# Packed bf16 down weights by converting DMAs, three down products per group moved forward, the verdict counted in two parts and the last output cut in the middle, in a state-space and fp8 FFN kernel

## Chip, cores and metric

The kernel runs on one core of a Trainium2 chip. The metric is the device time of one execution in microseconds (us). A core has five engines with instruction streams of their own: TensorE (matmuls; PE in the profile, its weight loads PEld), VectorE (DVE), ScalarE (ACT), GpSimd (POOL) and SyncE (SP). They run side by side and wait for each other through semaphores. DMAs are issued by SP (its queue is q1 in the profile) and by POOL (q0), and 16 DMA engines serve both queues.

## The reference

x has the shape (B, H, L) = (128, 32, 512) in f32. The reference computes

```
K    = state-space kernel, (H, L), from log_dt, C, log_A_real, A_imag   # 64 complex modes
y    = causal convolution of x[:, h, :] with K[h] + x * D, masked to length[b]
g, u = fp8(y) @ gate_w.T * s_g,  fp8(y) @ up_w.T * s_u        # 512 -> 1376, fp8(): clip to +-448, round to e4m3
hid  = silu(g) * u
out  = x + fp8(hid) @ down_w.T * s_d                          # 1376 -> 512
```

The three weights hold fp8 values, stored as f32 with one scale each.

## The kernel before, in words

The 32 heads are worked in G = 8 groups of HG = 4 heads, 512 (head, row) columns per group. I = 1376 is padded to IC = 11 chunks of 128. The program first makes the convolution kernels K in three batches of heads (class `Powers`), writes them to DRAM (`kpad`) and reads them back, per head, as Toeplitz tiles `st` (`toeplitz`, L475 and L476).

One group goes through these stages:

- `conv` (L572): for each head 6 f32 matmuls with `st` (L490 to L499), then VectorE writes the masked fp8 tile `q` (L576, L586). `sort` (L589) permutes the rows by length on TensorE, and ScalarE copies the result to `qs` (L601).
- `gate_up` (L630): for each of the 11 chunks 4 gate and 4 up matmuls (L646), ScalarE's silu (L654), VectorE's product `v` (L656). Chunks are quantised in batches of one or two (`quantise`, L615): ScalarE's magnitude `m` (L621), then three VectorE steps (L622, L623, L624) that write the bf16 tile `hq`. There are seven such jobs. Three are done inside `gate_up`, the other four are put between the convolutions of the next group, and the last two of these cover chunks 9 and 10.
- `Down` (L672): for each head 11 matmuls `dp` (L689), one per chunk, with a [128, 128] piece of `hq` as weights and 512 columns of `dm` as moving data; `put_out` (L698) adds the scaled result to `xn` on VectorE (L702) and sends rows to `out` with an indirect DMA on POOL's queue (L707).

The order is written out by hand: `with after(x)` puts what follows behind `x` on its engine. In group g's loop body (from L765), after `gate_up` of group g, TensorE gets: two convolutions of group g+1; chunks 0 to 4 (EARLY = 5) of heads 0 and 1; the other two convolutions and sorts; chunks 5 to 8 (LATE = 9) of heads 0 and 1; two sorts; chunks 0 to 8 of head 2 (L818); and then, at L819 to L825, chunks 9 and 10 of heads 0, 1 and 2 and all 11 of head 3. Chunk 10 waits for the last quantisation job. In group G-2 = 6 head 3 is left for the next group's time (L831). The last group's head 3 is worked in two halves of 256 columns (`halves`, L764), its products come batch by batch (L840 to L850), and `verdict` is put behind the third head's.

The PSUM tiles have tags with two banks each: `gp`, `up`, `cp`, `dp`. In `Down` heads 0 and 1 use `dp`, heads 2 and 3 use `cp` (as the convolutions do).

Weights: gate, up and down are loaded as f32 with SP's DMAs and stay in SBUF (`gw`, `uw`, `dw`). As all values fit in bf16, matmuls read the upper halves with a step of two bf16 (L570). down is loaded behind x of group 1 in two parts (L740, L741). The assumption is checked: `low_halves` (L535) lets ScalarE sum the lower halves of each chunk (4 + 4 + 11 sums, four per group from group 0 on, L805), and `verdict` (L548) collects these sums and checks of overflow, equal scales and row counts in the tile `ok`; a matmul with `ones` (L561) adds up over partitions, and `any_bad` (L562) is loaded by all engines (L923). If it is set, the slow path `wide` runs, else all engines branch past it (L924) to the end of the program (L970).

Besides, POOL issues the loads of `xs` (L111, and L112, which accumulates), the gathers of `xn` (L464), and in group 0 the write of `kpad` for batch 1 (L334) and the `st` loads of group 1.

## Time and profile before

| | us |
|---|---|
| median of 3 runs | 305.42 (304.99 to 305.79) |
| profiled execution | 304.11 |
| its span, from the first to the last instruction | 302.3 |
| DVE busy | 264.3 (87% of the span) |
| PE busy | 282.8 (94%) |
| ACT busy | 180.9 (60%) |
| POOL busy | 51.1 (17%) |
| granted TensorE clock, mean | 0.989 |

The profile is of one execution. Its page gives the busy time of each engine, the chain of work that ended last, the costliest groups of instructions and the DMAs. The trace behind it answers finer questions: the chain in order of time, timelines of one engine in a window (start, us, what, count, idle time before and who ended it), waits, and the instructions of one line or tile. A busy PE isn't PE at its peak: matmuls are pipelined, so the record of one is longer than its distance to the next. Instructions of the sequencers (waits, branches, register loads; SPq, PEldq) are not counted as busy.

### The profile page before, as it was taken

The numbers are of one execution on the slowest core, as the hardware profiler recorded it, in microseconds if no ns is written. First come the engines' busy times: TensorE is split into PE (matmuls) and PEld (weight loads), VectorE is DVE, ScalarE is ACT, GpSimd is POOL, SyncE is SP. The second block draws the span as 40 slices with busy tenths as digits, with TensorE's granted clock in tenths as the row PEclk, the third lists the DMA queues.
The fourth block names the chain that finished last, engine by engine and source line by source line (L and its number), as shares of the span: only waits on it lengthen the run. The fifth ranks groups of instructions, "written<-read, shape, count | busy, mean of one in ns | idle before, by whom it ended". The sixth has DMA issues, their size and how long they took to land.

```text
span 302.3 us, 4827 instructions
## 1 busy us (share of the span) xinstructions
PE 282.8 (94%) x1691; PEld 171.6 (57%) x1708; DVE 264.3 (87%) x466; ACT 180.9 (60%) x385; POOL 51.1 (17%) x105
## 2 busy tenths in 40 slices
PE   8999999997999999999999999999999999999940
PEld 3477567454774557645774567555774567455420
DVE  5875999989999999969997899969996999899970
ACT  5964882977739783657736782738523891579200
POOL 5771440210002100030002100310003100010030
PEclk9999999999999999999999999999999999999995
DMA  2599999970159603793149503890259530020031
GB/s 82 200 264 382 380 360 348 269 280 18 28 133 252 252 1 58 183 304 127 29 133 265 239 1 89 236 327 12 57 133 300 184 129 0 0 105 3 0 128 55
DMA packets 26119, 47.95 MB, mean 159 GB/s; under 512 B 2864, under 2 KB 15420, under 8 KB 24296
## 3 DMA queue, kind: packets, MB, share of 16 engines
q1 hardware_dynamic: 21784, 26.28, 29.4%
q0 software_dynamic: 4304, 21.29, 20.2%
q8 instruction: 15, 0.25, 0.3%
q14 instruction: 16, 0.13, 0.1%
HBM read 39.03 MB, written 8.54 MB: 157 GB/s over the span
## 4 chain that ended last, share of the span: by engine, by line
DVE 45%; PE 28%; issue 12%; ACT 8%; DMA 3%; SPq 1%; POOL 1%; ACTq 0%; POOLq 0%
DVE v L656 11%; DVE v L622 11%; PE dp L689 10%; DVE hq L623 10%; PE gp L646 5%; DVE q L576 5%; ACT s L654 5%; PE up L646 4%; DVE hq L624 4%; ACT m L621 2%; DVE xn L702 2%; DMA st<-kpad 2%; PE cp L497 1%; PE cp L495 1%; PE cp L496 1%
## 5 line engine op out<-in xcount | busy, mean ns | idle before, releaser
L689 PE MATMUL dp<-dw,hq 128*128 128x512 bf16 (+1 forms) x347 | 81.1, 380 | 2.5 <-DVE hq L624 0.8
L654 ACT ACTIVATE s<-gp,psc 128x512 f32<-128x512 f32 x88 | 58.4, 679 | 30.7 <-PE gp L646 30.4
L646 PE MATMUL up<-qs,uw 128*128 128x512 fp8e4 (+1 forms) x352 | 70.3, 322 | 2.3 <-DVE v L656 1.8
L656 DVE SCALAR_TENSOR_TENSOR v<-up,psc,s 128x512 f32<-128x512 f32 x88 | 64.5, 747 | 7.7 <-ACT s L654 7.7
L646 PE MATMUL gp<-qs,gw 128*128 128x512 fp8e4 (+1 forms) x352 | 70.5, 322 | 0.6 <-ACT qs L601 0.6
L689 PEld LDWEIGHTS <-hq 128*128 128x128 bf16 x363 | 33.3, 96 | 42.5 <-DVE hq L624 5.2
L623 DVE SCALAR_TENSOR_TENSOR hq<-m,v 128x1024 bf16<-128x1024 bf16 (+1 forms) x56 | 55.6, 993 | 1.1
L622 DVE SCALAR_TENSOR_TENSOR v<-m,v 128x1024 f32<-128x1024 bf16 (+1 forms) x56 | 55.4, 990 | 1.2 <-ACT m L621 1.2
L621 ACT ACTIVATE m<-v 128x1024 bf16<-128x1024 f32 (+1 forms) x56 | 48.7, 870 | 8.9 <-DVE v L656 8.9
L646 PEld LDWEIGHTS <-uw 128*128 128x128 bf16 x352 | 32.1, 97 | 28.9 <-issue 3.8
L646 PEld LDWEIGHTS <-gw 128*128 128x128 bf16 x352 | 31.9, 97 | 26.4 <-issue 0.7
L601 ACT ACTIVATE qs<-pq 128x376 fp8e4<-128x376 f32 x32 | 14.6, 479 | 29.7 <-PE pq L593 29.7
L702 DVE SCALAR_TENSOR_TENSOR xn<-dp,nsc,xn 128x512 f32<-128x512 f32 (+1 forms) x33 | 23.0, 730 | 8.8 <-PE dp L689 8.8
L493 ACT ACTIVATE shared<-sp,inv 128x128 f32<-128x128 f32 x32 | 11.3, 360 | 27.6 <-PE sp L490 27.6
L576 DVE SCALAR_TENSOR_TENSOR q<-cp,inv,shared 128x512 fp8e4<-128x512 f32 x32 | 23.8, 744 | 1.5 <-PE cp L499 1.0
L707 POOL DMA_INDIRECT out<-xn,index x10 | 10.5, 1051 | 75.4 <-DVE xn L702 71.9
L111 POOL DMA_DIRECT2D xs<-xT x6 | 3.5, 586 | 116.4 <-PE sp L490 116.4
L624 DVE TENSOR_SCALAR hq<-hq 128x1024 bf16<-128x1024 bf16 (+1 forms) x56 | 20.9, 373 | 1.4
L495 PE MATMUL cp<-st,xg 128*128 128x256 f32 x64 | 19.2, 381 | 0.0
L497 PE MATMUL cp<-st,xg 128*128 128x256 f32 x64 | 19.1, 381 | 0.0
L496 PE MATMUL cp<-st,xg 128*128 128x256 f32 x64 | 19.0, 380 | 0.0
L607 ACT ACTIVATE s<-q 128x1024 bf16<-128x1024 fp8e4 x16 | 16.7, 1054 | 0.0
(159 smaller groups left out, 283.6 us busy)
## 6 DMA issues: line engine op xcount, KB each, us to landing
xg<-xT SPq DMA_DIRECT2D x8, 1024.0 KB, 7.4
st<-kpad SPq DMA_DIRECT2D x28, 192.0 KB, 3.8
st<-kpad SPq DMA_DIRECT2D x28, 128.0 KB, 4.0
xs<-xT POOLq DMA_DIRECT2D x12, 256.0 KB, 5.3
dw<-downT SPq DMA_DIRECT2D x2, 1280.0 KB, 19.8
gw<-gateT SPq DMA_DIRECT2D x2, 768.0 KB, 8.2
gw<-gateT SPq DMA_DIRECT2D x1, 1216.0 KB
uw<-upT SPq DMA_DIRECT2D x1, 1216.0 KB, 15.2
```

Of the source, the lines that this page charges most:

```text
L495: nc.tensor.matmul(cp[:, 1:4:2, :], xg[:, 0, b], st[:, 2:4, :], start=True, stop=False)
L497: nc.tensor.matmul(cp[:, 1:3, :], xg[:, 1, b], st[:, 3:5, :], start=False, stop=False)
L576: nc.vector.scalar_tensor_tensor(q[:, j, :].rearrange("p (k c l) -> p k c l", k=2, c=2), cp.rearrange("p (k c) l -> p k c l", k=2), inv[:, ...
L621: nc.scalar.activation(m, v, AF.Abs, scale=2.0**20 * (1.0 + 2.0**-6), accum_out=acc)
L622: yield nc.vector.scalar_tensor_tensor(v, m, 1.5 * 2.0**14, v, ALU.max, ALU.add)
L623: yield nc.vector.scalar_tensor_tensor(out, m, 1.5 * 2.0**14, v, ALU.max, ALU.subtract)
L624: yield nc.vector.tensor_scalar(out, out, FP8_MAX, -FP8_MAX, ALU.min, ALU.max)
L646: multiplied = nc.tensor.matmul(o[:, :, 0 : CAPS[c]], w[:, c, i * P : (i + 1) * P], qs[:, :, OFF[c] : OFF[c] + CAPS[c]], start=(c == 0), s ...
L654: gated = nc.scalar.activation(s, gp, AF.Silu, scale=pgate)
L656: done = nc.vector.scalar_tensor_tensor(v[:, (i - i0) * T : (i - i0 + 1) * T], up, pup, s, ALU.mult, ALU.mult)
L689: done = nc.tensor.matmul(self.dps[n], self.hq[:, i, j * B : (j + 1) * B], dm[:, i, l0:l1], start=(i == 0), stop=(i == IC - 1),)
L702: added = nc.vector.scalar_tensor_tensor(o, self.dps[n], ndown, o, ALU.mult, ALU.add)
```

## The change

- `dw` (f32) becomes `dm` (bf16, packed). POOL loads it with DMAs that convert f32 to bf16: chunks 0 to 4 behind the write of `kpad` of batch 1, then the `st` loads of the four heads of group 1, then chunks 5 to 10. SP no longer loads down there.
- For the check of the lower halves, f32 chunks of down are loaded once more into a staging tile of four buffers (`stage_down`), on SP's queue behind x of group g+2 in groups 1, 2 and 3. ScalarE sums them there, as many sums as before.
- In groups 0 to 5, chunks 0 to 2 of head 3 are multiplied right behind head 2's chunks 0 to 8 (`ahead`), and are left out of head 3's later run.
- `verdict` is divided: `hold_others` counts all checks but `big` behind the first of the last group's remaining jobs, where group 6's last output is put too; `hold_big` counts `big` behind the last job; the matmul over partitions comes behind the first head's products, and `all_hold` compares behind the second head's output.
- The last group's output is sent as heads 0 and 1 and heads 2 and 3, where it was heads 0 to 2 and head 3.

The diff, without the slow path `wide`, which now loads down itself:

```diff
@@ -128,20 +128,22 @@
     x0 = load_x(0)
     gw = const.tile([P, LC, IP], F32, name="gw")
     uw = const.tile([P, LC, IP], F32, name="uw")
-    dw = const.tile([P, IC, L], F32, name="dw")
+
+    dm = const.tile([P, IC, L], BF16, name="dw")
     FI = I // P
 
     def load_gate_up(w, src, i0, i1, queue=nc.sync):
         return queue.dma_start(w[:, :, i0:i1], src[:, i0:i1].rearrange("(c p) i -> p c i", p=P))
 
-    def load_down(i0, i1, queue=nc.sync):
+    def load_down(w, i0, i1, queue):
         if i0 < FI:
-            queue.dma_start(
-                dw[:, i0 : min(i1, FI), :],
+            done = queue.dma_start(
+                w[:, 0 : min(i1, FI) - i0, :],
                 downT[i0 * P : min(i1, FI) * P, :].rearrange("(c p) l -> p c l", p=P),
             )
         if i1 > FI:
-            queue.dma_start(dw[0 : I - FI * P, FI, :], downT[FI * P :, :])
+            done = queue.dma_start(w[0 : I - FI * P, FI - i0, :], downT[FI * P :, :])
+        return done
 
 
     I1, I2, IH = 2 * P, 3 * P, 6 * P
@@ -434,7 +436,7 @@
         if IP > I:
             nc.gpsimd.memset(gw[:, :, I:], 0.0)
             nc.gpsimd.memset(uw[:, :, I:], 0.0)
-            nc.gpsimd.memset(dw[I - FI * P :, FI, :], 0.0)
+            nc.gpsimd.memset(dm[I - FI * P :, FI, :], 0.0)
         for kt in kts[1:]:
             nc.gpsimd.memset(kt, 0.0)
         nc.gpsimd.tensor_scalar(number, col_f[:, B:], -1.0, B - 1.0, ALU.mult, ALU.add)
@@ -535,31 +537,67 @@
     def low_halves(pool):
 
         n = 0
-        for w in (gw, uw, dw):
-            F = w.shape[2]
-            for c in range(w.shape[1]):
-                junk = pool.tile([P, T], F32, name="s")
-                nc.scalar.activation(
-                    junk.bitcast(U8)[:, 0:F], w.bitcast(U16)[:, c, 0 : 2 * F : 2], AF.Copy, accum_out=low[:, n : n + 1]
-                )
+
+        def summed(w, F, rows=P):
+            junk = pool.tile([P, T], F32, name="s")
+            return nc.scalar.activation(
+                junk.bitcast(U8)[0:rows, 0:F],
+                w.bitcast(U16)[0:rows, 0 : 2 * F : 2],
+                AF.Copy,
+                accum_out=low[0:rows, n : n + 1],
+            )
+
+        for w in (gw, uw):
+            for c in range(LC):
+                yield summed(w[:, c, :], IP)
                 n += 1
-                yield
-
-    def verdict(behind):
-        nf, nb, nl = fin.shape[1], big.shape[1], low.shape[1]
-        ok = chk.tile([P, nf + nb + nl + LC], F32, name="ok")
-        nc.vector.tensor_scalar(ok[:, 0:nf], fin, 3.0e38, None, ALU.is_lt)
-        nc.vector.tensor_scalar(ok[:, nf : nf + nb], big, 3.0e38, None, ALU.is_lt)
-        nc.vector.tensor_scalar(ok[:, nf + nb : nf + nb + nl], low, 0.0, None, ALU.is_equal)
-        nc.vector.tensor_copy(ok[:, nf + nb + nl : nf + nb + nl + 1], same)
-        nc.vector.tensor_scalar(ok[:, nf + nb + nl + 1 :], fits[:, 0, :], 0.0, None, ALU.is_gt)
-        bad = chk.tile([P, 1], F32, name="bad")
-        nc.vector.tensor_reduce(bad, ok, AX.X, ALU.min)
-        nc.vector.tensor_scalar(bad, bad, -1.0, 1.0, ALU.mult, ALU.add)
-        bp = ps.tile([1, 1], F32, name="bp", tag="cp")
-        with after(behind):
-            nc.tensor.matmul(bp, ones, bad, start=True, stop=True)
-        nc.vector.tensor_scalar(any_bad, bp, 0.0, None, ALU.is_gt)
+        for c in range(IC):
+            yield summed(staged[c], L, min(P, I - c * P))
+            n += 1
+
+    staged = []
+
+    def stage_down(pool, n):
+
+        for c in range(len(staged), min(IC, len(staged) + n)):
+            w = pool.tile([P, 1, L], F32, name="wd", bufs=n)
+            load_down(w, c, c + 1, nc.sync)
+            staged.append(w[:, 0, :])
+
+
+    count = chk.tile([P, 2], F32, name="count")
+
+    def hold(n, parts):
+
+        ok = chk.tile([P, sum(v.shape[1] for v, *_ in parts)], F32, name=f"ok{n}")
+        c0 = 0
+        for v, limit, op in parts:
+            c1 = c0 + v.shape[1]
+            alone = dict(accum_out=count[:, n : n + 1]) if len(parts) == 1 else {}
+            done = nc.vector.tensor_scalar(ok[:, c0:c1], v, limit, *((0.0, op, ALU.add) if alone else (None, op)), **alone)
+            c0 = c1
+        if len(parts) > 1:
+            done = nc.vector.tensor_reduce(count[:, n : n + 1], ok, AX.X, ALU.add)
+        return c0, done
+
+    def hold_others():
+        return hold(0, [
+            (fin, 3.0e38, ALU.is_lt), (low, 0.0, ALU.is_equal), (same, 1.0, ALU.is_equal), (fits[:, 0, :], 0.0, ALU.is_gt)
+        ])
+
+    def hold_big():
+        return hold(1, [(big, 3.0e38, ALU.is_lt)])
+
+    def verdict():
+        bp = ps.tile([1, 2], F32, name="bp", tag="cp")
+        return bp, nc.tensor.matmul(bp, ones, count, start=True, stop=True)
+
+    def all_hold(bp, n):
+
+        both = chk.tile([1, 2], F32, name="both")
+        nc.vector.tensor_scalar(both, bp, -1.0, None, ALU.mult)
+        nc.vector.tensor_tensor(both[:, 0:1], both[:, 0:1], both[:, 1:2], ALU.add)
+        nc.vector.tensor_scalar(any_bad, both[:, 0:1], float(-P * n), None, ALU.is_gt)
 
     def narrow():
         with ExitStack() as arm:
@@ -567,11 +605,11 @@
             yp = arm.enter_context(tc.tile_pool(name="yp", bufs=2))
             hp = arm.enter_context(tc.tile_pool(name="hp", bufs=2))
             vp = arm.enter_context(tc.tile_pool(name="vp", bufs=3))
-            gm, um, dm = (w.bitcast(BF16)[:, :, 1::2] for w in (gw, uw, dw))
-
-            def conv(g, q, j, xg, xs, before):
-
-                st, loaded = toeplitz(stp, g * HG + j, nc.gpsimd if g == 1 else nc.sync)
+            gm, um = (w.bitcast(BF16)[:, :, 1::2] for w in (gw, uw))
+
+            def conv(g, q, j, xg, xs, before, k=None):
+
+                st, loaded = k or toeplitz(stp, g * HG + j)
                 cp, t, convolved, copied = convolve(st, xg, xs, j, inv[:, 0:1], before)
                 nc.vector.scalar_tensor_tensor(
                     q[:, j, :].rearrange("p (k c l) -> p k c l", k=2, c=2),
@@ -677,9 +715,12 @@
                     self.between, self.some = between, some
                     self.dps = [None] * len(units)
 
-                    n, last = len(units) - 1, (HG - 1) * L
+                    n = len(units) - 1
                     k = g + max(0, g - (G - 2))
-                    self.sent = [(k, HG - 2, 0, last), (k + 1, n, last, HG * L)] if g >= G - 2 else [(g, n, 0, HG * L)]
+                    m = HG - 2 if g == G - 2 else HG - 3
+                    self.sent = [(g, n, 0, HG * L)]
+                    if g >= G - 2:
+                        self.sent = [(k, m, 0, (m + 1) * L), (k + 1, n, (m + 1) * L, HG * L)]
 
                 def multiply(self, n, i0, i1):
                     j, l0, l1 = self.units[n]
@@ -737,10 +778,16 @@
                 loaded = load_gate_up(uw, upT, IH, I)
             with after(loaded):
                 x_next = load_x(1)
-                load_down(0, EARLY)
-                load_down(EARLY, IC)
             with after(done):
-                others[0].response(made, nc.gpsimd)
+                *_, written = others[0].response(made, nc.gpsimd)
+            ks = []
+            with after(written):
+                down_there = load_down(dm, 0, EARLY, nc.gpsimd)
+            for j in range(HG):
+                with after(ks[-1][1] if ks else down_there):
+                    ks.append(toeplitz(stp, HG + j, nc.gpsimd))
+            with after(ks[-1][1]):
+                load_down(dm[:, EARLY:, :], EARLY, IC, nc.gpsimd)
             to_index = indices(done)
             next(to_index)
             with after(done):
@@ -786,7 +833,7 @@
                         with after(done):
                             *_, done = jobs.pop(0)
                     with after(last), after(done):
-                        last, done, loaded, sent = conv(g + 1, q, j, xg, xs, sent)
+                        last, done, loaded, sent = conv(g + 1, q, j, xg, xs, sent, ks.pop(0) if ks else None)
                     if j == 1:
                         for n in range(2):
                             with after(last):
@@ -797,6 +844,8 @@
                 with after(loaded):
                     if g + 2 < G:
                         x_next = load_x(g + 2)
+                    if g:
+                        stage_down(vp, 4)
                 if g + 2 < G:
                     xs_next, summed = load_sums(g + 2)
                 with after(summed):
@@ -816,11 +865,17 @@
                         *_, done = job
                 with after(last):
                     last = d.multiply(2, 0, LATE)
+
+
+                ahead = 3 if g < G - 2 else 0
+                if ahead:
+                    with after(last):
+                        last = d.multiply(HG - 1, 0, ahead)
                 for n in range(HG):
                     if (g, n) == (G - 2, HG - 1):
                         break
                     with after(last):
-                        last = d.multiply(n, LATE if n < 3 else 0, IC)
+                        last = d.multiply(n, LATE if n < HG - 1 else ahead, IC)
                     with after(done):
                         done = d.put_out(n)
                 if g == 0:
@@ -832,11 +887,16 @@
             check_q(G - 1, q)
             before = d
             d = Down(g, hq, xn, halves, ["dp", "gp", "up", "gp", "up"])
-            for job in jobs:
+            for n, job in enumerate(jobs):
                 with after(done):
                     *_, done = job
+                if not n:
+                    with after(done):
+                        done = before.put_out(HG - 1)
+                    with after(done):
+                        n0, done = hold_others()
             with after(done):
-                done = before.put_out(HG - 1)
+                n1, done = hold_big()
             for i0, i1 in ((0, EARLY), (EARLY, LATE)):
                 for n in range(len(halves)):
                     with after(last):
@@ -844,16 +904,24 @@
             for n in range(len(halves)):
                 with after(last):
                     last = d.multiply(n, LATE, IC)
-                    if n == len(halves) - 2:
-                        with after(done):
-                            verdict(last)
-                d.put_out(n)
+                with after(done):
+                    done = d.put_out(n)
+                if n == 0:
+                    with after(last):
+                        bp, last = verdict()
+                if n == 1:
+                    with after(done):
+                        all_hold(bp, n0 + n1)
 
...
@@ -958,7 +1026,7 @@
     groups = np.split(a["x"].reshape(B, H * L), H // 4, axis=1)
     arrays |= {f"x{g}": v for g, v in enumerate(groups)}
     arrays = {k: np.ascontiguousarray(v) for k, v in arrays.items()}
-    widths = [*(v.shape[1] for v in groups[:-2]), 3 * L, L, 3 * L, L]
+    widths = [*(v.shape[1] for v in groups[:-2]), 3 * L, L, 2 * L, 2 * L]
 
     nc = bacc.Bacc("TRN2", target_bir_lowering=False, num_devices=1)
     args = {
```

More of the change, by code (lines that the diff above doesn't have):

```diff
@@ L856, in wide @@
             wp2 = arm.enter_context(tc.tile_pool(name="wp2", bufs=2))
+            dw = wp.tile([P, IC, L], F32, name="wdw")
+            if IP > I:
+                nc.vector.memset(dw[I - FI * P :, FI, :], 0.0)
+            load_down(dw, 0, IC, nc.sync)
             masks = [wp.tile([P, LC, B], F32, name=f"mask{n}") for n in range(2)]
@@ L863, in quantise @@
                 nc.vector.tensor_scalar(v, v, FP8_MAX, -FP8_MAX, ALU.min, ALU.max)
-                m = wp2.tile([P, 4 * T], F32, name="wm")
+                m = wp2.tile([P, 4 * T], F32, name="wm", bufs=1)
                 nc.scalar.activation(m[:, 0:F], v, AF.Copy, scale=2.0**20)
```

## The prediction

> **What bounds the kernel now.** I read the page first, then the chain of work that ended last in order of time, then the timelines of TensorE, VectorE and the weight loads for one middle group, and the end of the program by its source lines.
>
> ```profile
> span 302.3 us, 4827 instructions
> ...
> DVE 45%; PE 28%; issue 12%; ACT 8%; DMA 3%; SPq 1%; POOL 1%; ACTq 0%; POOLq 0%
> ```
>
> VectorE and TensorE share the chain, and neither rests: a middle group takes 33.29 us (its first gate product starts at 165.82, 199.11 and 232.40 in the chain). The two hand over once per group. From the chain:
>
> ```profile
> 194.24 0.70 DVE hq L623
> 195.32 3.79 PE dp L689 x16
> 199.11 0.64 PE gp L646 x4
> ```
>
> The last quantisation step (L624, ends 195.26) frees chunk 10 of hq; TensorE then runs the 16 down products left, and only then the next gate product, on which VectorE's next group depends. VectorE's side of it (start, us, [idle before]):
>
> ```profile
> 194.97 0.29 DVE L624 TENSOR_SCALAR hq<-hq 128x512 bf16<-128x512 bf16 x1
> 195.76 2.07 DVE L702 SCALAR_TENSOR_TENSOR xn<-dp,nsc,xn 128x512 f32<-128x512 f32 x3 [0.50 <-PE dp L689]
> 199.15 0.75 DVE L702 SCALAR_TENSOR_TENSOR xn<-dp,nsc,xn 128x512 f32<-128x512 f32 x1 [1.32 <-PE dp L689]
> 200.56 0.75 DVE L656 SCALAR_TENSOR_TENSOR v<-up,psc,s 128x512 f32<-128x512 f32 x1 [0.67 <-ACT s L654]
> ```
>
> It idles 1.32 and 0.67 us behind those products. From 200.56 to 228.55 it idles only 0.52 us. So a shorter hand-over shortens the group, as long as TensorE reaches it in time. In this group it does, with little to spare: its last product before the wait starts at 194.80, the next could start at 195.02 and starts at 195.32. TensorE's slack is 0.29 us (0.60 in group 0, 0.14 in group 2, 0.23 in group 6).
>
> **Packed down weights, the product itself.** Now each product reads every second bf16 of dw. Two rows give the spacing of 512-column bf16 products, strided and packed:
>
> ```profile
> 223.91 1.96 PE L689 MATMUL dp<-dw,hq 128*128 128x512 bf16 x8
> ...
> 13.69 2.75 PE L233 MATMUL nothing<-still 128*128 128x512 bf16 x12
> ```
>
> One strided product takes 387 ns from start to end, so the spacing is (1.96 - 0.387)/7 = 0.225 us; a packed one at full clock takes 380 ns, (2.75 - 0.38)/11 = 0.215. Single records give 226 and 216 ns. I take 10 ns per product, 44 products in a group: 0.44 us of TensorE's time. Bounds: nothing (the difference comes from something other than the stride) and 10 ns, since gate products (L646) with packed moving data are spaced 215 ns too.
>
> [...]
>
> **Three chunks of the fourth head moved forward** (groups 0 to 5). Products after the wait: 13 instead of 16, so 13 x 0.216 = 2.81 instead of 3.63 us, 0.82 less. Before the wait TensorE has three products more (0.65) and saves 10 ns on 28 (0.28): it arrives 0.37 later, less the slack of 0.29 is 0.08 late. Net 0.74 per group. The other way round, TensorE's period falls from 33.29 - 0.29 = 33.00 by 0.44 to 32.56: 0.73. The fourth product's PSUM bank comes from "cp": its previous user is read by VectorE at 224.17 to 224.92, three us before it is wanted, so that adds no wait. By group:
> - Group 0: nothing. Its output steps alternate with the angles of batch 2, and VectorE is busy from 58.64 to 66.8, then waits 1.21 us for ScalarE's sines; TensorE isn't on that path.
> - Groups 1 and 2 together: VectorE is continuous from 67.97 to 93.87, so group 1 gains 0.74 at its gate products alone. In group 2 the chain is TensorE throughout. TensorE comes 0.74 + 0.28 - 0.65 = 0.37 earlier (128.36), VectorE saves its one idle of 0.39 (128.43). Products then start at 128.48 and gate products at 131.29, where now they would stand at 132.35 without the gate product that was put ahead: 1.05.
> - Groups 3 to 5: 3 x 0.74 = 2.2. Group 6, nothing moved: 5 products x 10 ns = 0.05.
> Sum 3.3 us.
>
> **The end.** Not the last output's landing but TensorE's instruction stream ends the program:
>
> ```profile
> L923 PEldq TENSOR_LOAD <-any_bad x1: 1109/1109/1109, 293.1 to 293.1; - x1
> ...
> L924 PEldq COMPARE_BRANCH  x1: 3938/3938/3938, 294.3 to 294.3; - x1
> ...
> L970 SPq DRAIN  x3: 7/7/7, 298.8 to 301.7; - x3
> ...
> L970 PEldq DRAIN  x2: 8/8/8, 301.4 to 301.8; - x2
> ```
>
> any_bad is written at 293.01; the load of it takes 1.1 us, the branch past `wide` 3.9, another 3.1 pass until TensorE's drain at 301.43. SyncE, which waits for the outputs, is there at 298.8. So an earlier verdict counts, and the last output has some 2.6 us of cover. After the change (times of before): the fourth head's output (0.68) and four counts with a reduction (some 0.5) go between quantisation jobs, so the last L624 ends at 288.55 + 1.17 = 289.73; `hold_big` (0.18) lies in the wait for the first product; outputs 0 and 1 at 290.22 and 290.89, ending 291.56; three small instructions of 0.09 spacing, as in the present `verdict`: any_bad at 291.84, 1.17 earlier. The output's last half is issued at 293.35 instead of 292.80 and is 512 instead of 256 KB (128 packets of 0.17 us on 16 engines, 1.4 us instead of 0.7): it lands about 1.2 later, and SyncE at 300.0 stays before TensorE's 300.26. GpSimd's own drain ends at 299.72 now and can move by 0.35 to 1.1. I take 1.0, bounds 0.5 and 1.2.
>
> **The converting load, in group 0.** dw now goes on SP's queue behind x of group 1:
>
> ```profile
> dw<-downT SPq DMA_DIRECT2D x2, 1280.0 KB, 19.8
> ```
>
> It lands just ahead of its first use (part one 46.08, product 46.59). After, GpSimd issues part one at 29.1, behind kpad; its queue's packets start some 4 us after issue (kpad 28.05 to 32.8). All 16 engines are full until 50 us, so bytes are not added, only reordered: x of group 1 (lands 38.8, wanted by TensorE at 42.41 and VectorE at 43.50) and the filters st (land 40.8 to 46.8, wanted 42.41 to 50.98) now share with part one. No row shows a converting packet. Bounds per 2 KB row: 84 ns (plain packet of SP's queue) and 178 ns (accumulating packet of xs, GpSimd's queue). Part one is 40 rows per engine, part two 46. At 84 ns x lands at 40 to 42, st from 40, part one by 40, part two by 49 against 53.2: cost nothing. At 178 ns, if a packet holds two rows against one of SP's, x lands near 46, 2.5 us late, and part two near 58.3 against 55.7, less the slack of 0.6 another 2.0: 4.5 us. I take nothing: accumulating reads two sources, twice the bytes, which alone explains twice 84 ns, while converting reads one. GpSimd's last filter load may wait for part one's landing (its issues eight apart share a semaphore in the trace), which delays its gather of xn (wanted 58.64) by 4 us from 51.1: still covered.
>
> **Other edits.** The 11 staged f32 chunks are 2.8 MB more on SP in groups 1 to 3: 1 MB is 2.8 us at 380 GB/s, in groups where the engines are half idle (DMA share 0.50 of 33.30 us); the next filters, behind them on SP, are issued 20 us ahead of use. Without that cover, 2.8 us a group. Chunks 4 to 10 wait on SP for ScalarE's sums of chunks before, about 3 us, under the same cover. ScalarE's 11 sums (0.62 + 0.19 each) stay. Cost 0, bound 1.
>
> **Sum.** 3.3 + 1.0 = 4.3 us. The profiled execution took 304.11 (span 302.3 and 1.8 around it): 299.8. The median of the three runs is 305.42, 1.3 above it: 301.1.
>
> **Rivals.**
> - *Slow conversion (slower).* In group 0 x, st and part two come late, and VectorE waits at add_chunks. At 178 ns a row 305.4 + 4.5 - 4.3 = 305.6; it decides from there: at 200 ns both parts take 2 us more, some 307.5. For: reading the xs row as the price of any arithmetic in a DMA, and the full engines up to 50 us. Against: bytes read. Chance 0.17.
> - *Half of it.* Conversion at 110 to 140 ns with two rows a packet: x 1 to 2.5 us late, 302 to 305, middle 303. Chance 0.14.
> - [...] Spacing stays 226 ns. Then the forward chunks come 0.68 - 0.29 = 0.39 late out of 0.68 won: 0.29 a group, 1.2 in all with groups 1 and 2, and 1.0 at the end: 303.2. The two spacings speak against it. Chance 0.08.
> - *The earlier verdict doesn't do what it says*, since GpSimd's drain or the larger last output ends the program: 302.1. Chance 0.06.
> - *Forecast*: 0.55, its own range 299.6 to 302.2.
>
> **Numbers.** 0.3% is 0.92 us, about what a measurement here can tell from no change. Faster: 0.55 + 0.10 (half) + 0.08 + 0.06 = 0.79; within: 0.04 + 0.03 = 0.07; slower 0.14. Range: 299.6 up to 305.0, which leaves out the slow conversion (0.17) and little else.
>
> **What would show it.** Spacing of L689 at 216 ns; 13 products between the last L624 and the next gate product in groups 0 to 5; groups 3 to 5 of some 32.55 us; any_bad some 1.2 us earlier than the shift of the last gate product. Wrong if VectorE idles before xs at about 43 us, if TensorE idles before L689 near 46 or 53 us on a DMA, or if the group stays at 33.

## The result, and the profile after

The changed kernel takes 300.18 us (median, 299.79 to 300.49) beside 305.25 for the kernel before on the same chip: ratio 0.983, 95% interval 0.981 to 0.985. In a second series (run `changed_again`, below) it took 300.57 beside 304.43: 0.987, interval 0.985 to 0.990. The forecast was 301.1 (range 299.6 to 305.0). Its sum was made against the profiled execution: 304.11 - 4.3 = 299.8; the profiled execution of the changed kernel took 300.10, with a span of 298.2 instead of 302.3 us.

From the page of the changed kernel, the span and the engines' shares of the chain that ended last:

```profile
span 298.2 us, 4854 instructions
...
PE 47%; DVE 30%; issue 8%; ACT 7%; DMA 2%; POOL 1%; SPq 1%; POOLq 0%; ACTq 0%
```

Before, VectorE led this chain with 45%. Now TensorE does. The hand-over of the same middle group, in the chain in order of time (start, us, what):

```profile
191.10 5.56 PE dp L730 x25
196.66 0.64 PE gp L684 x4
```

There is no step of VectorE ahead of the products any more: they run through to the next gate product. (One of the 26 has no record.) VectorE's side of it, from its timeline:

```profile
193.19 0.29 DVE L662 TENSOR_SCALAR hq<-hq 128x512 bf16<-128x512 bf16 x1
194.11 2.07 DVE L743 SCALAR_TENSOR_TENSOR xn<-dp,nsc,xn 128x512 f32<-128x512 f32 x3 [0.62 <-PE dp L730]
196.70 0.75 DVE L743 SCALAR_TENSOR_TENSOR xn<-dp,nsc,xn 128x512 f32<-128x512 f32 x1 [0.52 <-PE dp L730]
198.11 0.75 DVE L694 SCALAR_TENSOR_TENSOR v<-up,psc,s 128x512 f32<-128x512 f32 x1 [0.67 <-ACT s L692]
```

The last quantisation step ends at 193.48, 13 products start behind it, and the gate product follows 3.2 us later in the chain; before it was 3.8. (The chain counts a piece from the end of the one before it; in the table below a product counts from its own start, 0.16 earlier.) VectorE's idle of 1.32 us before the fourth output is 0.52 now. The spacing of the down products, from a run of 26 in TensorE's timeline of `changed_again` (the same program):

```profile
190.78 5.77 PE L730 MATMUL dp<-dw,hq 128*128 128x512 bf16 x26
```

One product takes 379 ns, so the spacing is (5.77 - 0.379)/25 = 0.216 us; it was 0.225. The converting load, from the page's list of DMA issues (two parts, KB written, us from issue to landing):

```profile
dw<-downT POOLq DMA_DIRECT2D x2, 640.0 KB, 11.8
```

And the end, by source lines (duration in ns, start):

```profile
L991 PEldq TENSOR_LOAD <-any_bad x1: 483/483/483, 289.7 to 289.7; - x1
...
L992 PEldq COMPARE_BRANCH  x1: 3918/3918/3918, 290.3 to 290.3; - x1
...
L1038 POOLq DRAIN  x3: 46/103/5406, 291.5 to 297.9; - x3
...
L1038 PEldq DRAIN  x2: 8/8/8, 297.3 to 297.7; - x2
```

The load of any_bad takes 0.48 us instead of 1.11, the branch 3.9 as before. GpSimd's drain starts at 291.52 and takes 5.41, so it ends at 296.93, only 0.4 before TensorE's at 297.34. Before, it ended 1.7 ahead.

The start of each group's first gate product (us). The row of the forecast is its gain added up: 0 for group 0, 0.74 and 1.05 after groups 1 and 2, then 0.73 a group, 0.05 for group 6.

| group | 0 | 1 | 2 | 3 | 4 | 5 | 6 | 7 |
|---|---|---|---|---|---|---|---|---|
| before | 28.03 | 61.83 | 97.56 | 132.35 | 165.66 | 198.95 | 232.24 | 262.97 |
| changed (first profile) | 28.80 | 61.78 | 96.25 | 131.40 | 163.95 | 196.50 | 229.04 | 259.73 |
| `changed_again` | 28.05 | 61.66 | 96.13 | 131.29 | 163.84 | 196.38 | 228.93 | 259.62 |
| gain of `changed_again` | 0.0 | 0.2 | 1.4 | 1.1 | 1.8 | 2.6 | 3.3 | 3.35 |
| gain as forecast | 0.0 | 0.0 | 0.7 | 1.05 | 1.8 | 2.5 | 3.25 | 3.3 |

(132.35 is worked out as in the prediction; one gate product stood ahead there.) From group 3 on the two rows agree within 0.1 us. In groups 1 and 2 they don't, and that is what most experiments are about. The remaining gain, from group 7's gate product to the end of the span, is 39.29 - 38.44 = 0.85 in the first profile and 0.56 in `changed_again`; forecast was 1.0.

### The profile page after: what moved, and what is told of

Read it like the earlier page. It is cut to its first block, busy times and chain, and to the rows that moved or that the text cites. A ratio compares the mean times of both kernels' runs of the same rounds, so it can differ in the third digit from the quotient of the medians.

```text
span 298.2 us, 4854 instructions
## 1 busy us (share of the span) xinstructions
PE 279.0 (94%) x1691; PEld 172.4 (58%) x1708; DVE 264.2 (89%) x468; ACT 180.5 (61%) x385; POOL 55.6 (19%) x108
## 4 chain that ended last, share of the span: by engine, by line
PE 47%; DVE 30%; issue 8%; ACT 7%; DMA 2%; POOL 1%; SPq 1%; POOLq 0%; ACTq 0%
PE dp L730 16%; DVE v L694 9%; PE up L684 7%; DVE v L660 6%; PE gp L684 6%; DVE hq L661 5%; ACT s L692 4%; PE cp L497 4%; PE cp L499 4%; PE cp L498 3%; DVE xn L743 3%; PE sp L492 2%; DVE hq L662 2%; DMA st<-kpad 2%; ACT m L659 2%
## 5 line engine op out<-in xcount | busy, mean ns | idle before, releaser
L730 PE MATMUL dp<-dw,hq 128*128 128x512 bf16 (+1 forms) x347 | 77.1, 372 | 3.2 <-DVE hq L662 2.2
L730 PEld LDWEIGHTS <-hq 128*128 128x128 bf16 x363 | 34.1, 98 | 38.8 <-DVE hq L662 4.9
```

The costliest lines, as they stand in the source:

```text
L730: done = nc.tensor.matmul(self.dps[n], self.hq[:, i, j * B : (j + 1) * B], dm[:, i, l0:l1], start=(i == 0), stop=(i == IC - 1),)
```

## The experiments

Each ratio is to the kernel before, run on the same chip in the same series; brackets are 95% intervals. Only `strided_sp`, `late_dm` and `verdict_first` ran in one series with the control `changed_again`. The others had no run of the changed kernel beside them: they are compared with it by their ratios, and stage by stage by the profiles, each of which is one execution.

| run | median us | ratio |
|---|---|---|
| `ahead0` | 302.72 | 0.994 [0.992, 0.996] |
| `strided` | 304.38 | 1.001 [0.998, 1.004] |
| `sines_first` | 301.47 | 0.990 [0.988, 0.992] |
| `old_end` | 300.86 | 0.988 [0.986, 0.990] |
| `changed_again` | 300.57 | 0.987 [0.985, 0.990] |
| `strided_sp` | 301.94 | 0.992 [0.990, 0.994] |
| `late_dm` | 300.20 | 0.987 [0.984, 0.989] |
| `verdict_first` | 299.62 | 0.984 [0.982, 0.987] |
| `few_steps` | 300.06 | 0.986 [0.984, 0.987] |
| `three_outs` | 300.22 | 0.986 [0.984, 0.987] |
| `ahead5` | 300.65 | 0.986 [0.984, 0.987] |
| `combined` | 299.30 | 0.981 [0.979, 0.984] |

### The control

> The changed kernel itself, once more, so that the other runs stand beside it on one chip: ratio 0.983 to the kernel before. Its profile also shows how much group 0 varies between executions of the same program: of five profiles with the converting load, TensorE waited 0.5 to 1.15 us near 37 us for the last part of the up weights in three.

0.987, a smaller gain than the 0.983 of the first series; the two intervals meet at 0.985. The gain is 3.9 to 5.1 us, and the profiles say 4.0. TensorE's longest wait in group 0:

```profile
37.31 0.81 PE L684 MATMUL up<-qs,uw 128*128 128x512 fp8e4 x4 [0.83 <-DMA uw<-upT]
```

The first profile doesn't have it, but there group 0 started 0.75 later (its first filters landed later). Of nine profiles with the converting load at its place, seven show this wait, of 0.5 to 1.15 us; the two without it are the two that started at 28.8. (Of the five that the expectation counts, one, `strided`, has a plain load.)

Behind that wait, x of group 1 was late too. The chain of `changed_again` around 43 us goes through its load (start, us from issue to landing):

```profile
25.92 17.30 DMA xg<-xT
```

TensorE idles 0.14 us for it, and so it does in `ahead5`, where the load takes 17.33. In the other five of the seven the chain up to 47 us goes through the up weights.

### No product moved forward

```diff
-                ahead = 3 if g < G - 2 else 0
+                ahead = 0
```

> The changed kernel without the three products moved forward (ahead = 0), everything else as changed. Theory A (the forecast's steps, group 0 gains nothing): 16 x 0.216 = 3.46 us of products behind the last quantisation step instead of 2.81, so groups 3 to 5 take 33.29 - 0.16 = 33.13 us instead of 32.55 (3 x 0.58 = 1.7) and groups 1 and 2 together some 0.65 more: 302.5. Theory B (what the two traces suggest): without the move the planner puts ScalarE's three sines of batch 2 ahead of the magnitude m of group 1's first batch again, as in the kernel before, and VectorE idles another 1.2 to 1.4 us at about 67 us: 303.8. Rival (packing alone makes the gain, the move none): 300.2.

302.72 is near theory A's figure, but the profile shows the step that theory B names. Groups 4 and 5 take 33.23 and 33.07 us (forecast for packing alone 33.13), and in group 1 VectorE waits for m. Its timeline in `ahead0`:

```profile
69.32 0.69 DVE L660 SCALAR_TENSOR_TENSOR v<-m,v 128x512 f32<-128x512 bf16 x1 [1.07 <-ACT m L659]
```

In the instruction order ScalarE's three sines stand ahead of m again, and group 1 takes 35.49 instead of 34.47. From group 0's to group 7's gate product `ahead0` takes 234.75 us, `changed_again` 231.57: 3.2 more, of which 1.0 in group 1, 1.0 in group 0, 1.2 in groups 4 and 5, and nothing in groups 2 and 3 together (67.68 and 67.71). So leaving the move out costs 2.0 to 3.3 us by the ratios and 3.2 by the profile, beside A's 2.3 and B's 3.6 (both counted from 300.2); the times alone don't decide between them. The 1.0 in group 0 isn't shown to come from the edit: the profiled execution is the slowest of six (303.5), and TensorE's wait for the up weights is 0.3 longer in it than in `changed_again`.

### The old order of the sines, forced

```diff
-                nc.scalar.activation(m, v, AF.Abs, ...)
+                with after(behind) if behind else ExitStack():
+                    nc.scalar.activation(m, v, AF.Abs, ...)
...
-                        others[1].sines()
+                        sines_2 = others[1].sines()
```

(`behind` is `sines_2` for the first batch of group 1.)

> The changed kernel with one order forced: ScalarE does the three sines of batch 2 ahead of the magnitude m of group 1's first batch, as the kernel before did; nothing else moves but the neighbouring silu and m of that group. Theory B (this order is worth over a microsecond): VectorE idles some 1.2 us near 67.5 us for m, its last quantisation step of group 1 ends 1.2 to 1.4 later than 93.24, TensorE has 0.15 us of slack there and then never waits again, so the delay stays to the end: 301.3 to 301.5. Theory A (that wait stood beside other work, so group 0 to 1 gained for another reason): 300.2.

301.47, where B put it. VectorE at the first quantisation step of group 1 in the kernel before:

```profile
67.97 0.69 DVE L622 SCALAR_TENSOR_TENSOR v<-m,v 128x512 f32<-128x512 bf16 x1 [1.21 <-ACT m L621]
```

ScalarE in the changed kernel does m first, and then the sines:

```profile
65.94 0.63 ACT L659 ACTIVATE m<-v 128x512 bf16<-128x512 f32 x1
...
66.57 0.43 ACT L278 ACTIVATE ang<-ang 128x272 f32<-128x272 f32 x1
```

VectorE around that step, first in the changed kernel, then in `sines_first`:

```profile
66.78 0.74 DVE L694 SCALAR_TENSOR_TENSOR v<-up,psc,s 128x512 f32<-128x512 f32 x1
67.44 0.67 DVE L660 SCALAR_TENSOR_TENSOR v<-m,v 128x512 f32<-128x512 bf16 x1
```

```profile
66.66 0.73 DVE L695 SCALAR_TENSOR_TENSOR v<-up,psc,s 128x512 f32<-128x512 f32 x1
68.30 0.69 DVE L661 SCALAR_TENSOR_TENSOR v<-m,v 128x512 f32<-128x512 bf16 x1 [0.92 <-ACT m L660]
```

Group 1 takes 35.47 us instead of 34.47, all other groups from 2 on are the same within 0.02. So 1.0 us of the gain is a change of order that the diff doesn't contain: `sines` has no place fixed against m. The planner, the step of the build that orders the instructions of each engine where `after` leaves the order open, now puts m first; without the moved products (`ahead0`) it puts the sines first again. Why it decides so isn't shown. In `sines_first` group 3's gate product starts at 132.28, where the kernel before had 132.35: without the new order, next to nothing was won up to there.

### The batch's product steps taken out of group 1's outputs

```diff
-... 1: (itertools.chain(others[1].coefficients(), others[1].products()), 5)}
+... 1: (others[1].coefficients(), 3)}
...
+                    list(others[1].products())
                     others[1].response()
```

> The changed kernel with the six product steps of the last convolution-kernel batch (two of 0.7 us, four of 0.42) taken out from between group 1's output steps; they are issued with that batch's response, so the planner puts them between the v and quantisation steps of group 2. Theory G (in group 2 the shorter hand-over ran into these steps: VectorE did 2.8 us of them before the first v, and TensorE's second up product waited 0.66 us for that v's PSUM bank): the wait is gone and group 2 takes some 34.4 us instead of 35.15, 0.7 us in all. Rival 1 (VectorE has to do them somewhere and TensorE is waiting for it all the same, later in group 2): no change within 0.2 us. Rival 2 (the 17 small kernel matmuls come later, behind group 2's gate and up products, and delay the response and the filters of a later group): slower.

What the theory named, in TensorE's timeline of the changed kernel (second line, first profile), and the same wait a group earlier (first line, `changed_again`):

```profile
65.85 0.80 PE L684 MATMUL up<-qs,uw 128*128 128x512 fp8e4 x4 [0.84 <-DVE v L694]
...
100.26 0.80 PE L684 MATMUL up<-qs,uw 128*128 128x512 fp8e4 x4 [0.66 <-DVE v L694]
```

In `few_steps` the second wait is gone: the first v of group 2 starts 1.95 us behind group 2's gate product instead of 3.21, and group 2 takes 34.11 instead of 35.15 us. But group 1 takes 34.95 instead of 34.47: TensorE waits 0.62 at 70.80 for another v. ScalarE's order there is that of the changed kernel. It is VectorE that has one of the product steps, which the planner has put between the quantisation steps of group 1 and ahead of that v:

```profile
69.20 0.68 DVE L312 TENSOR_TENSOR ang<-ang,mag 128x512 f32<-128x512 f32 x1
...
70.00 0.74 DVE L694 SCALAR_TENSOR_TENSOR v<-up,psc,s 128x512 f32<-128x512 f32 x1
```

In `changed_again` that v stands at 69.50, without this step ahead of it. So the steps moved not only into group 2, as the expectation has it, but also a group ahead; and one of 0.7 us still stands ahead of the first v of group 2 (97.85). Net 0.55 of 0.7 us by the profile; by the ratios 0.5, with overlapping intervals.

### Five products moved forward

```diff
-                ahead = 3 if g < G - 2 else 0
+                ahead = 5 if g < G - 2 else 0
```

> The changed kernel with five instead of three products of the fourth head moved forward. Theory A' (after the change TensorE doesn't wait in groups 1 to 5, its last-needed hq step ends 0.15 us before TensorE comes to it): nothing is left to fill, period 32.55 us as before, no change within 0.2 us. Rival (the hand-over is still the bound, and 11 products behind the wait instead of 13 save 0.43 us a group): 2 us faster.

Steady groups stay at 32.55: TensorE is the bound there, and the rival falls. What wasn't expected: groups 1 and 2 take 34.90 and 35.58, 0.43 more each, two products' worth. VectorE's first output behind group 1, and TensorE's waits in groups 1 and 2, in `ahead5`:

```profile
94.62 0.75 DVE L743 SCALAR_TENSOR_TENSOR xn<-dp,nsc,xn 128x512 f32<-128x512 f32 x1 [1.05 <-PE dp L730]
```

```profile
66.28 0.80 PE L684 MATMUL up<-qs,uw 128*128 128x512 fp8e4 x4 [1.27 <-DVE v L694]
...
101.01 0.80 PE L684 MATMUL up<-qs,uw 128*128 128x512 fp8e4 x4 [1.09 <-DVE v L694]
```

With three products (`changed_again`) that idle was 0.62, and the two waits were 0.84 and 0.66. What is moved ahead of the first head's last products delays the first output, and behind the outputs VectorE has the batch's steps and then the v that TensorE waits for. The medians don't show this 0.9 us: the ratio is 0.986, that of the control in another series 0.987.

### Down read with a step of two, twice

First with the plain f32 load at the converting load's place, then on SP's queue where the kernel before had it; all other order as changed, no staged chunks:

```diff
-    dm = const.tile([P, IC, L], BF16, name="dw")
+    dw = const.tile([P, IC, L], F32, name="dw")
...
-            gm, um = (w.bitcast(BF16)[:, :, 1::2] for w in (gw, uw))
+            gm, um, dm = (w.bitcast(BF16)[:, :, 1::2] for w in (gw, uw, dw))
...
-                down_there = load_down(dm, 0, EARLY, nc.gpsimd)
+                down_there = load_down(dw, 0, EARLY, nc.gpsimd)     # strided
+                load_down(dw, 0, EARLY, nc.sync)                    # strided_sp, behind x of group 1
```

> The changed kernel with down kept as f32 in SBUF and read with a step of two bf16, loaded by plain DMAs at the same places of GpSimd's queue; the order of all products and of ScalarE's work is that of the changed kernel, and the staged f32 chunks are left out, since the checked sums read the resident weights. Theory A (a strided product costs 10 ns more): spacing 226 ns again, TensorE's 44 products of a group 0.44 us longer, and as TensorE doesn't wait in groups 1 to 5 these take 33.0 us: 5 x 0.44 = 2.2, in all 302.4. Rival 1 (the step is free and the shorter spacing came from the order): spacing 216 ns, 300.2. Rival 2 (converting packets or the staged chunks cost something that is hidden in the result): below 302.0 although the spacing is 226 ns, with x of group 1 or the filters of group 1 landing earlier than in the changed kernel.

> The changed kernel with down kept as f32, read with a step of two bf16, and loaded by SP behind x of group 1 as the kernel before did (no staged chunks, no converting load; all other orders as changed). Theory A (10 ns a strided product is all that packing gives): products 226 ns apart, groups 1 to 5 0.3 to 0.44 us longer each, 2.0 in all, and group 0 about 0.3 longer: 2.0 to 2.3 us over the changed kernel. Theory F (the plain load at the converting load's place made the other strided kernel so slow, as x of group 1 landed at 45.3 instead of 41.7): here x lands near 39, TensorE doesn't wait for it, and the kernel is some 2 us faster than that one. Rival (the strided read costs 4 us whatever the load): as slow as that one, 1.001 of the kernel before. Rival 2 (the converting load itself costs up to 1 us in group 0, through the wait for the up weights): only 1.2 to 1.5 us over the changed kernel.

`strided` lost the whole gain, and what goes beyond theory A's 2.2 us is not the stride. TensorE in group 0 of `strided`:

```profile
45.44 0.67 PE L497 MATMUL cp<-st,xg 128*128 128x256 f32 x2 [1.19 <-DMA xg<-xT]
```

x of group 1 landed 17.7 us after its issue here. In the seven profiles with a converting load at that place that show x's landing it took 15.0 to 17.5 us, in `strided_sp` and in the kernel before 12.9. So in these profiles a load of down on GpSimd's queue ahead of x's landing went with a later x. That the plain load (packets of 4 KB, 171 ns each in the median) is worse than the converting one (96 ns) isn't shown: in `ahead0`, with the converting one, x took 17.45 and group 0 34.58 us, no less than the 34.38 of `strided`, and x landed 0.14 us before TensorE used it. Part of the late landing is a late issue (27.59, in those seven 25.9 to 26.7). The changed kernel stands at the edge over which `strided` falls. Against the first profile of the changed kernel, group 0 of `strided` is 1.4 us longer and starts 0.9 later (29.71), which isn't explained; its runs spread from 303.2 to 307.0. `strided_sp` is 2.4 us faster than `strided` at 301.94, 1.4 over the control: theory F, and rival 2's figure. Its products:

```profile
191.60 6.03 PE L730 MATMUL dp<-dw,hq 128*128 128x512 bf16 x26
```

(6.03 - 0.387)/25 = 0.226. Groups 3 to 5 take 32.99 instead of 32.55, groups 1 and 2 0.32 more each: 2.0 us for the stride. Group 0 takes 0.42 less than in `changed_again` (33.20 instead of 33.62), without the wait for the up weights; beside the other profiles that start before 28.4 and have the load at its place (33.32 to 33.57, `changed_again` apart) it is 0.1 to 0.4 less. So packing gains 2.0, and its load costs some 0.1 to 0.4 by these profiles of one execution each.

### The converting load later

```diff
-            with after(written):
-                down_there = load_down(dm, 0, EARLY, nc.gpsimd)
             for j in range(HG):
-                with after(ks[-1][1] if ks else down_there):
+                with after(down_there if ks else written):
                     ks.append(toeplitz(stp, HG + j, nc.gpsimd))
+                down_there = ks[-1][1]
+                if j == 0:
+                    with after(down_there):
+                        down_there = load_down(dm, 0, EARLY, nc.gpsimd)
```

> The changed kernel with the first part of the converting load behind the two filter loads of group 1's first head instead of ahead of all of them; nothing else moves. Theory F (the early converting load takes turns of the DMA engines from SP's queue, and the up weights and x come late): up weights land near 36 as in the kernel before, TensorE's wait near 37 us is gone, 0.3 to 0.6 us faster than the changed kernel in the median. Rival (group 0 is bound by VectorE and the wait is hidden): no change within 0.2 us. Rival 2 (part one then lands after 46.6 us, where its first product wants it): slower, by as much as it is late.

The wait for the up weights (0.83 us in `changed_again`) is gone; part one lands at 44.4, before its first use at 47.1. Group 0 takes 33.34 instead of 33.62, 0.3 less. But `old_end`, with the load at its place and a wait of 0.54, took 33.32. The medians differ by 0.4, which their intervals don't separate from none. So it is shown that the load makes the up weights late; what this costs lies between nothing and 0.4.

### The old end

```diff
-widths = [..., 3 * L, L, 2 * L, 2 * L]
+widths = [..., 3 * L, L, 3 * L, L]
```

(with the old `verdict` and group 6's output behind all jobs.)

> The changed kernel with the old end: group 6's last output and one verdict behind all quantisation jobs, the comparison behind the third head's product, outputs cut as heads 0 to 2 and head 3. Theory A (the end as forecast, an earlier verdict and nothing else): any_bad 1.2 us later relative to the last gate product, span 1.0 longer, 301.2. Theory C (from the two traces): any_bad only 0.15 later relative to the last gate product, since the three small steps of the new verdict stand between outputs, but the stretch from any_bad to the end 0.7 longer: 301.0. Rival (the end of the outputs, not the verdict, ends the program): 300.2 or less.

By the ratios 0.2 to 1.5 us slower, too wide to size it. By the profile the stretch from group 7's gate product to the end is 39.50 us, in the changed kernel's two profiles 38.44 and 38.73. any_bad is written 30.04 behind that product (changed: 29.89), and from there to the end 9.46 pass (changed: 8.55 and 8.84). That is theory C: the load of any_bad takes 1.10 on TensorE here, 0.48 there. By source lines, `old_end` (the changed kernel's line stands in the section on the result):

```profile
L998 PEldq TENSOR_LOAD <-any_bad x1: 1095/1095/1095, 289.4 to 289.4; - x1
```

The rest is within what varies from execution to execution: from the end of TensorE's branch to its drain 2.9 to 3.7 us pass in the fourteen profiles.

### The verdict's steps together

```diff
                 if n == 1:
                     with after(done):
-                        all_hold(bp, n0 + n1)
+                        done = all_hold(bp, n0 + n1)
```

> The changed kernel with the three small steps of the verdict together ahead of the third head's last output step, where the planner had put output steps between them: any_bad is written some 0.9 us earlier, the last output step ends 0.2 later. Theory D (two streams end the program: TensorE's, 7.7 us behind any_bad, and GpSimd's drain, 1.75 us behind the last output's landing): TensorE is done at 296.4, GpSimd's drain still at some 297.0, so the end moves by 0.2 at most: within 0.3 us of the changed kernel. Rival (TensorE's stream alone, as the forecast had it): 0.9 us faster.

What was in the way, in VectorE's timeline of the changed kernel:

```profile
288.30 0.14 DVE L598 TENSOR_SCALAR both<-bp 1x2 f32<-1x2 f32 x1
288.37 0.73 DVE L743 SCALAR_TENSOR_TENSOR xn<-dp,nsc,xn 128x512 f32<-128x512 f32 x1
289.03 0.14 DVE L599 TENSOR_TENSOR both<-both 1x1 f32<-1x1 f32 x1
289.10 0.47 DVE L743 SCALAR_TENSOR_TENSOR xn<-dp,nsc,xn 128x256 f32<-128x256 f32 x1
289.49 0.13 DVE L600 TENSOR_SCALAR any_bad<-both 1x1 int32<-1x1 f32 x1
```

Output steps fill the gaps between the three small steps. In `verdict_first` any_bad is written at 288.83, and of the drains

```profile
L1038 POOLq DRAIN  x3: 46/103/5020, 291.9 to 297.5; - x3
...
L1038 PEldq DRAIN  x2: 8/8/8, 296.5 to 297.3; - x2
```

GpSimd's (291.91 + 5.02 = 296.93, behind the last landing at 295.16) is now later than TensorE's at 296.55. From group 7's gate product to the end 38.00 us pass, 0.44 and 0.73 less than in the changed kernel's profiles; the median is 0.95 lower, with overlapping intervals. Counted from that product, GpSimd's drain ends at 37.17 as before (37.20 and 37.17), TensorE's starts at 36.79 instead of 37.61 and 37.89. The end moved by the distance between the two. In all fourteen profiles the span ends 0.83 or 0.84 us behind the later of these two drains. So theory D's mechanism is right, and its 0.2 was too small: it took GpSimd's drain to come later, which it didn't, and the distance of one profile.

### The last output in three parts

```diff
+                    if g == G - 1:
+                        self.sent = [(k, 1, 0, 2 * L), (k + 1, 2, 2 * L, 3 * L), (k + 2, n, 3 * L, HG * L)]
```

(on top of `verdict_first`.)

> The changed kernel with the verdict's three small steps together (as in verdict_first) and the last group's output sent in three parts, heads 0 and 1, head 2, head 3. Theory D (in verdict_first GpSimd's drain, 1.75 us behind the last output's landing, ends the program, TensorE's stream being done 0.4 us before it): the last part is 256 instead of 512 KB, it lands 0.4 to 0.7 us earlier, and the end moves by the 0.4 us up to TensorE's stream: 0.2 to 0.4 us faster than verdict_first. Rival (a third issue of 0.96 us on GpSimd delays the last one, and the landing goes by the issue, not by the bytes): not faster than verdict_first, or slower by up to 0.5.

The rival: the last part is issued 0.82 later (291.37 instead of 290.55) and lands at 295.20 instead of 295.16, counted from group 7's gate product 0.09 earlier. Nothing is won: in this execution TensorE's drain (297.41) is again the later one, as 3.7 us pass behind its branch.

### Together

> What the runs pointed to, together, on the changed kernel: the verdict's three steps together (verdict_first), part one of the converting load behind the first head's filters (late_dm), the product steps of the last batch out of the output steps (few_steps), and in group 0 one product of the fourth head moved forward instead of three, since ahead5 showed that the outputs, and behind them the first v of group 1, come later by each product that is moved ahead of them there (two more products: group 1 and group 2 0.43 us longer each). Theory: the parts add up, 0.4 (TensorE's wait for the up weights gone) + 0.5 (group 2) + 0.5 (end) + 0.4 (group 1: gate products 0.43 later, but TensorE's wait of 0.84 for the first v gone): 1.8 us below the changed kernel, ratio 0.981 to the kernel before. Rival (the parts stand in each other's way: what group 0 and 1 gain is waited for in the next group's v): 0.984, no better than verdict_first alone.

299.30, 0.981 as the theory had it, below both kernels; its interval ends below that of `changed_again` (0.985) and overlaps that of the first series. The sum came out, its parts did not. In its profile groups 0 to 2 take 102.3 us (`changed_again` 103.2, the first profile 102.6). Group 0 takes 33.66, no less than `changed_again`: TensorE doesn't wait for the up weights, but 0.49 for the last quantisation step. Group 1 takes 34.52 (`changed_again` 34.47, `few_steps` 34.95), where 0.4 less was counted; group 2 takes 34.12, 1.0 less where 0.5 was counted; the end takes 37.9, 0.6 to 0.9 less where 0.5 was counted.

## Why the prediction was right, point by point

- **Spacing 216 ns: right, and worth what was said.** 0.44 us in each steady group, shown by `strided_sp`, where the step of two bf16 brings 226 ns back. So the rival with a spacing that stays at 226 ns falls. Why a step of two costs these 10 ns isn't shown.
- **Steady groups of 32.55 us: right** (32.55 in all), and so was the warning that TensorE comes late to the hand-over (in the changed kernel's profiles the last quantisation step ends 0.20 us before the first product that needs it starts; 0.06 in the kernel before): it is the bound now, and `ahead5` wins nothing there.
- **Group 0 gains nothing: right in the sum to its end (0.2), wrong in what follows.** "VectorE ... then waits 1.21 us for ScalarE's sines" was taken as fixed. The wait went, since the planner turned the order of m and sines: 1.0 us (`sines_first`).
- **Groups 1 and 2 gain 1.05: the sum is right by luck.** "In group 2 the chain is TensorE throughout" failed, and so did the 0.74 of group 1. With gate products earlier, VectorE's small steps between the output steps stood ahead of the first v, and TensorE waited for it, 0.84 in group 1 and 0.66 in group 2; the kernel before has neither wait. Group 2 takes 35.15 where 34.47 was forecast. In `sines_first` the two groups take 70.62 us, in the kernel before 70.52: without the new order of m and sines nothing of the 1.05 is left. This loss and the new order cancel; neither was foreseen.
- **Group 6: 0.05, right** (30.69 against 30.73).
- **The end: 1.0 forecast, 0.85 and 0.56 measured, for another reason.** The last quantisation step came 1.17 later as worked out, but any_bad came only 0.15 earlier, not 1.17: "three small instructions of 0.09 spacing" was wrong, output steps were put between them. The rest came from the load of any_bad, 0.6 shorter, which no step named, and from what varies behind the branch. That GpSimd's drain may end the program was a rival; it is 0.4 us away, and past TensorE's once the verdict is early (`verdict_first`).
- **The converting load at nothing: nearly, at no more than 0.4 us.** 96 to 98 ns a row is near the 84 that was taken. But the forecast looked for its victims among x, the filters and part two, and the one that was late most often was the last part of the up weights, on SP's queue before them. x landed at 41.7 to 43.9, where 40 to 42 was forecast, and that is the edge: TensorE waited 0.14 us for it in two of the nine profiles. The slow rival's larger effect, x near 46 and TensorE waiting 1.2 us for it, was seen once, with the plain load (`strided`).
- **Staged chunks at nothing: right.** 49.4 instead of 48.0 MB are moved, and no engine waits for them.

The 4.3 us stand beside 4.0 in the profiles, and 3.9 to 5.1 in the medians. Of the 4.0, the steady groups (2.2) came as reasoned; groups 1 and 2 came to their sum by luck, and most of the end for another reason.

## What to carry to other kernels

Where a planner fills what the program leaves open, an edit also moves steps that the diff doesn't name: list each engine's order before and after, and put a price on each pair that has changed places. When a hand-over gets shorter, look at what the engine that hands over does next, as small steps that lay in the old wait now lie ahead of the next consumer. Here a load that moved to another queue made transfers late that the old queue still had in flight (TensorE waited 0.5 to 1.15 us for the up weights in seven of nine profiles): look for the victim among transfers issued before it too.

## What the runs showed of the hardware that was not expected

- The load of any_bad takes 1.05 to 1.16 us on all five engines in the kernel before and in `old_end`, where all start within 0.02 us. In the twelve other profiles GpSimd's starts 0.4 to 1.5 us later and takes 1.1 to 1.24; the other four take 0.46 to 0.55. That they disturb each other is only a guess from the order; no run tested it.
- GpSimd's drain ended 1.65 to 1.8 us behind the last output's landing in the kernel before, the changed kernel, `verdict_first` and `three_outs`.
- A converting row (2 KB read, 1 KB written) takes 96 to 98 ns of a DMA engine in the median, and a plain packet of two rows 171 (`strided`).
- The span ended 0.83 or 0.84 us behind the later of TensorE's and GpSimd's drain in all fourteen profiles.
- Group 0's first gate product started between 28.0 and 29.7 us, and in two executions of the same program at 28.05 and 28.80; in the later one a filter load on the chain took 5.8 instead of 5.1 us. What makes it vary stays open.
